# Leaving steps of a selective scan: clamp on VectorE, power first on GpSimd, gate ahead of the products

## The chip, the cores and the metric

One core of a Trainium2 chip runs the whole kernel. Its engines run side by side, each through its own queue in order: PE (TensorE, matrix products), DVE (VectorE), ACT (ScalarE), POOL (GpSimd) and SP (SyncE, which issues most DMAs). The metric is the device time of one execution in microseconds (us); the time shown for a kernel is the median of its runs.

## The reference

Eight images of 128 x 128 pixels with 128 channels go through two layers.

Layer 0 is linear attention: a projection to q, k and v, softmax of q over the head's dimension and of k over all pixels, a context matrix for each image, an output projection, a normalization over channels and a residual.

Layer 1 is a state-space block. `x @ Win` gives 256 channels `xb` and 256 gates `z`. `xb` goes through a 3 x 3 depthwise convolution and a SiLU. The result is read in four directions (by rows, backwards, by columns, columns backwards), and each direction has a scan over its 16384 positions:

```
state = exp(delta * A) * state + delta * u * B;   y = state * C
```

`delta` is a softplus of a small projection. The four directions' `y` are summed, with `u * D` added. What matters for the change is the end of the layer, for each pixel over its 256 channels:

```
yz  = y * silu(z)
var = mean(yz*yz) - mean(yz)^2             # over the channels
out = (gamma * (yz - mean) / sqrt(var + 1e-05) + beta) @ Wout
```

## The kernel before

Three stages run one after another: `layer0`, `layer1_front` (convolution, and all that the scans read, to DRAM) and `layer1_scan`. The change is in the last.

**Units and steps.** `layer1_scan` works through 512 units: eight output images, four directions each, 16 chunks of 1024 positions each. Channels lie on the 128 partitions, in two halves `c` = 0, 1. `step(n)` (L1100) issues unit n's scans, what follows the scans of unit n-1, and what leads to unit n+1. Everything is issued inside `in_order`, which ties each engine to the order in which `step` writes it: an engine never takes a later instruction first.

In a step without anything else, ACT makes the decay (`decay`, L937) and the softplus of the next unit (`soften`, L933); POOL multiplies u and delta into `h`, one half of the channels at a time (`weigh`, L946); DVE scans each half in place (`scan`, L954 forwards, L956 backwards); PE spreads C over the partitions into PSUM (`spread`, L962), once for each half chunk (512 positions); and DVE multiplies `h` by it (`emit`). For the first direction of an image the product writes straight into `y` (L974), the sum of the directions, which stays in SBUF for a whole image. For the other directions it takes three DVE operations (L984 or L988, `gather` L996, L977) and two additions on POOL (`add`, L1004).

`h` has two buffers, so `weigh(n, 0)` waits for the last reader of unit n-2's `h`: that is `scan(n-1, 1)`, which starts from its last column.

**Leaving steps.** When an image's four directions are summed, its 16 chunks leave, one a step, while the next image's first direction is scanned: steps 64 to 79 for the first image, and so on. The last image's chunks leave with no scan beside them. `leaving` says which chunk is at which step; in `step`, `now` is the chunk that leaves at this step, `last` the one before, `soon` the next. A chunk goes through this:

- `gate` (L1024) multiplies `y` by the stored `silu(z)`, in SBUF. Half 0 of a chunk is gated on POOL, at the end of the step before; half 1 on DVE, in the chunk's own step. (For the first chunk of an image both are on POOL.)
- `square` on ACT (L1027), `moments` on PE (L1037), `keep` on ACT (L1043), `to_tokens` on PE (L1049) and `square_mean` on ACT (L1053) give mean and mean square of each pixel.
- `variance` on DVE (L1057) subtracts the squared mean, from PSUM, at the end of the step, behind both scans. The tile `rstd` holds 8 values a partition.
- `project` on PE (L1069) multiplies the gated chunk by `Wout`, into the PSUM bank of the decay.
- `deviation(last)`, a step later, on POOL: the variance is clamped at 0 with 1e-5 added (L1061) and raised to the power -1/2 (L1062), in place.
- `store(last)` on DVE (L1075): eight instructions scale the projection by `rstd` and add the bias, into one of two buffers `r`, and SP sends each half chunk out (L1079).

So DVE's queue in a leaving step reads: product of the first half, gate of half 1, product of the other half, scan of half c = 0, eight store instructions, scan of c = 1, variance. POOL's reads: weighing c = 0, clamp, power, weighing c = 1, gate of the next chunk's half 0, and in two of three steps the issue of an accumulating DMA that adds `u * D` into `y` (`add_d`, L902). SP's reads: the rows of unit n+2 (L911, L912), z of a later chunk (L1020), `u` of unit n+2 in two halves (L918, each into a buffer that the weighing of unit n frees), and the two stores.

Of the kernel before, what the change touches and what calls it, by code (L numbers as in the profile page):

```python
# [11 lines left out]
ALU = mybir.AluOpType  # L12
# [22 lines left out]
EPS1 = 1e-5  # L35
# [707 lines left out]
def layer1_scan(ctx: ExitStack, tc, ubs, xps, zs, gs, dtw, dtb, a_log, gamma, beta, w_out, out):  # L743
# [15 lines left out]
    nc = tc.nc  # L759
# [144 lines left out]
    def load_rows(n):  # L904
        sl, i = units[n]
        m = sl.at(i)
        rw = rws[n % 3]
        md = NCH - 1 - m if sl.dt_turned_back else m
        src = xps[sl.dt_image, sl.dt_order].rearrange("j r l -> (j r) l")
        for j in range(3):  # L910
            nc.sync.dma_start(rw[3 * NR * j : 3 * NR * j + 3 * NR, :], src[:, md * CH : md * CH + CH])  # L911
        nc.sync.dma_start(rw[96:99, :], xps[sl.b, sl.order, :, R + 1, m * CH : m * CH + CH])  # L912

    def load(n, c):
        sl, i = units[n]
        m = sl.at(i)
        ubt[n, c] = wp.tile([P, CH], F32, name="ubt", tag="ub", bufs=4)
        nc.sync.dma_start(ubt[n, c], ubs[sl.b, sl.order, c][:, m * CH : m * CH + CH])  # L918
# [12 lines left out]
    def soften(n, c):  # L931
        sp[n, c] = t = wp.tile([P, CH], F32, name="sp", tag="sp", bufs=2)
        nc.scalar.activation(t, da[n, c], AF.Softplus)  # L933

    def decay(n, c):
        sl, i = units[n]
        nc.scalar.activation(da[n, c], sp[n, c], AF.Exp, scale=sa[:, sl.s, c : c + 1])  # L937

    def weigh(n, c):
        if c == 0:  # L940
            hs[n] = wp.tile([P, NC2, CH], F32, name="h", bufs=2)
        u, t, h = ubt.pop((n, c)), sp.pop((n, c)), hs[n][:, c, :]
        if units[n][0].permuted:
            u = u.rearrange("p (e h w) -> p h e w", e=2, w=W // 2)
            t, h = (v.rearrange("p (h e w) -> p h e w", e=2, w=W // 2) for v in (t, h))
        nc.gpsimd.tensor_tensor(h, u, t, ALU.mult)  # L946

    def scan(n, c):
        sl, i = units[n]
        x, e = da[n, c], hs[n][:, c, :]  # L950
        last = 0 if sl.back else CH - 1
        start = 0.0 if i == 0 else hs[n - 1][:, c, last : last + 1]
        if sl.back:
            nc.vector.tensor_tensor_scan(e[:, ::-1], x[:, ::-1], e[:, ::-1], start, ALU.mult, ALU.add)  # L954
        else:
            nc.vector.tensor_tensor_scan(e, x, e, start, ALU.mult, ALU.add)  # L956
# [7 lines left out]
    def emit(n, hf):  # L964

        sl, i = units[n]
        h = hs[n][:, :, hf * 512 : hf * 512 + 512]
        c = cps.pop((n, hf)).to_broadcast([P, NC2, GN])  # L970
        if sl.place == 0:
            v = sl.y_at(i, hf)
            split = "p c (a b) -> p c a b"
            nc.vector.tensor_tensor(v, h.rearrange(split, b=H), c.rearrange(split, b=H), ALU.mult)  # L974
            return
        if hf != sl.first:
            nc.vector.tensor_tensor(h, h, c, ALU.mult)  # L977
            return
        p = da.pop((n, 1))
        if sl.y_turned:  # L980
            ts[n] = p.rearrange("p (c b a) -> p c b a", c=NC2, a=GW)
            t = p.rearrange("p (c b a) -> p c a b", c=NC2, a=GW)
            split = "p c (a b) -> p c a b"
            nc.vector.tensor_tensor(t, h.rearrange(split, b=H), c.rearrange(split, b=H), ALU.mult)  # L984
        else:
            t = p.rearrange("p (c q) -> p c q", c=NC2)
            ts[n] = t.rearrange("p c (a b) -> p c a b", b=H)
            nc.vector.tensor_tensor(t, h, c, ALU.mult)  # L988

    def gather(n):  # L990

        sl, i = units[n]
        v = sl.y_at(i, sl.first)
        if sl.y_turned:
            v = v.rearrange("p c a b -> p c b a")
        nc.vector.tensor_tensor(v, v, ts.pop(n), ALU.add)  # L996
# [12 lines left out]
    def piece(m, hf):  # L1009
        return y[:, :, (2 * m + hf) * GN : (2 * m + hf + 1) * GN]  # L1010
# [5 lines left out]
    def fetch(o, m):  # L1016
        for hf in range(2):
            zt[m, hf] = z = wp.tile([P, NC2, GN], F32, name="z", bufs=6)
            p = mirrored(o, m, hf)
            nc.sync.dma_start(z, zs[o].rearrange("c p l -> p c l")[:, :, p * GN : p * GN + GN])  # L1020

    def gate(o, m, hf, eng):
        z, ym = zt[m, hf], piece(m, hf)
        eng.tensor_tensor(z, ym[:, :, ::-1] if o % 2 == 1 else ym, z, ALU.mult)  # L1024

    def square(m, hf):
        nc.scalar.activation(piece(m, hf), zt[m, hf], AF.Square)  # L1027

    def moments(m):

        pm = pe.tile([P, GN], F32, name="pm", tag="pt")
        for c in range(NC2):
            for j in range(2):
                for hf in range(2):
                    at = 32 * (2 * j + hf)
                    v = piece(m, hf) if j else zt[m, hf]
                    nc.tensor.matmul(pm[at : at + 32, :], mean, v[:, c, :], start=(c == 0), stop=(c == NC2 - 1))  # L1037
        pts[m, "rows"] = pm

    def keep(m):  # L1040
        pm = pts[m, "rows"]
        pts[m, "rows"] = sr = wp.tile([P, GN], F32, name="sr", bufs=1)
        nc.scalar.copy(sr, pm)  # L1043
# [11 lines left out]
    def variance(m):  # L1055
        rst[m] = rstd = sm.tile([P, GW, NC2], F32, name="rstd")
        nc.vector.tensor_tensor(rstd, pts.pop(m)[:, :, :, 1], mv.pop(m), ALU.subtract)  # L1057

    def deviation(m):
        rstd = rst[m]  # L1060
        nc.gpsimd.tensor_scalar(rstd, rstd, 0.0, EPS1, ALU.max, ALU.add)  # L1061
        nc.gpsimd.tensor_tensor(rstd, rstd, half, ALU.pow)  # L1062

    def project(m, hf, bank):
# [35 lines left out]
    def step(n):  # L1100
        live = 0 <= n < N
        then = n + 1 < N
        before = 1 <= n <= N
        now, last, soon, later = (leaving.get(n + i) for i in (0, -1, 1, 2))
        first = before and units[n - 1][0].place == 0
        if before:
            half1 = units[n - 1][0].first
            emit(n - 1, half1)
            if not first:
                gather(n - 1)  # L1110
        if now and last:
            gate(*now, 1, nc.vector)
        if before:
            emit(n - 1, 1 - half1)
        if n + 2 < N:
            load_rows(n + 2)
        if n in fetched:
            fetch(*fetched[n])
        if live:
            decay(n, 0)  # L1120
        if now:
            square(now[1], 1)
        if live:
            decay(n, 1)
            weigh(n, 0)
            if n + 2 < N:
                load(n + 2, 0)
        if last:
            deviation(last[1])
        if live:  # L1130
            weigh(n, 1)
            if n + 2 < N:
                load(n + 2, 1)
        if now:
            moments(now[1])
        if live:
            scan(n, 0)
            da.pop((n, 0))
        if last:
            for hf in range(2):  # L1140
                store(*last, hf)
        if then:
            for c in range(NC2):
                delta(n + 1, c)
        if now:
            keep(now[1])
        if then:
            soften(n + 1, 0)
        if now:
            to_tokens(now[1])  # L1150
            square_mean(now[1])
        if then:
            soften(n + 1, 1)
        if live:
            scan(n, 1)
        if first:
            hs.pop(n - 1)
        if now:
            variance(now[1])
        if live:  # L1160
            half1 = units[n][0].first
            spread(n, half1, "pc")
            spread(n, 1 - half1, "pt")
        if soon and now:
            gate(*soon, 0, nc.gpsimd)
        elif soon:
            gate(*soon, 1, nc.gpsimd)
        elif later:
            gate(*later, 0, nc.gpsimd)
        if soon:  # L1170
            square(soon[1], 0)
        if now:
            p = da.pop((n, 1)) if live else px.tile([P, CH], F32, name="px")
            for hf in range(2):
                project(now[1], hf, p[:, hf * 512 : hf * 512 + 512])
        elif live and units[n][0].place == 0:
            da.pop((n, 1))
        if before and not first:
            add(n - 1)
            hs.pop(n - 1)  # L1180
        if n in weighed:
            units[weighed[n]][0].weights()
        if n in summed:
            add_d(*summed[n])
# [78 lines left out]
```

## Time and profile before

| what | value |
|---|---|
| median of the runs shown (3) | 9363.71 us (9353.22 to 9363.73) |
| the profiled execution's own time | 9364.78 us |
| its span, first to last instruction | 9363.0 us |
| busy: PE / DVE / ACT / POOL | 6381.8 / 7997.6 / 7096.1 / 7319.3 us |
| scans: L954 and L956 | 1178.5 and 1177.8 us, 512 each, 2332 ns each |
| weighing: L946 on POOL | 2416.1 us, 1024, 2388 ns mean |
| gate: L1024 on DVE | 255.4 us, 120, 2128 ns mean; shortest 1214, longest 3367 |
| gate: L1024 on POOL | 329.7 us, 136, 2424 ns mean |
| clamp: L1061 on POOL | 143.3 us, 128; shortest 243, median 1209, longest 1640 ns |
| power: L1062 on POOL | 212.9 us, 128; 1657 to 1677 ns |
| variance: L1057 on DVE | 18.8 us, 128; 131 to 168 ns |

Busy time is the time in which an engine has an instruction under way; an instruction that has started and stands still counts as busy. The idle time before an instruction, with what ended it, stands behind it in square brackets. A row of a timeline with xN is N instructions on end.

From 5129 us on, the eight sets of leaving steps are where TensorE is busiest in the scan stage: 5129 to 5310, 5719 to 5900, 6306 to 6490, 6890 to 7070, 7473 to 7660, 8064 to 8250, 8655 to 8830, and the last image from 9233 to the end. In the first of them PE is busy for 146.70 of 181 us, DVE for 167.74, ACT for 139.09 and POOL for 155.81, and the DMA engines for a share of 0.89. A step of the other kind takes about 8.2 us (the first products L984 at 5328.88 and 5337.10).

### The profile page before, as it was taken

How to read it: one execution, taken by the hardware profiler on the slowest of the kernel's cores; microseconds unless marked ns; L12 is line 12 of the kernel's file. 1: busy time of each engine (PE TensorE's matmuls, PEld its weight loads, DVE VectorE, ACT ScalarE, POOL GpSimd, SP SyncE). 2: the span in 40 equal slices, each digit the busy share in tenths (PEclk: the TensorE clock that was granted, in tenths of full speed). 3: DMA queues.
4: the chain of work that ended last, by engine and by line, in shares of the span. 5: the costliest groups of instructions: out<-in, count | busy, mean ns of one | idle time of the engine just before them, and what ended most of it. 6: DMA issues, size and time to landing. Idle time of an engine off the chain costs nothing. (4 is left out here: it accounts for less than half of the span.)

```text
span 9363.0 us, 91413 instructions
## 1 busy us (share of the span) xinstructions
PE 6381.8 (68%) x24512; PEld 3145.7 (34%) x24512; DVE 7997.6 (85%) x7953; ACT 7096.1 (76%) x8066; POOL 7319.3 (78%) x4684
## 2 busy tenths in 40 slices
PE   8899998998888988888434636436364363643636
PEld 5555555554333333333101403114031140321403
DVE  6667666674799988888799999999999999999996
ACT  5555555658788888888688787887888878788885
POOL 3446444465688888888589899998999989999997
PEclk9999999999999999999655756657575575665857
DMA  1322333223477788888757759578595785967858
GB/s 75 144 91 90 134 118 144 105 80 143 159 240 239 249 233 230 234 233 225 215 155 208 234 169 260 166 204 239 167 267 166 206 234 165 252 175 200 248 165 216
DMA packets 934771, 1750.67 MB, mean 187 GB/s; under 512 B 150229, under 2 KB 376149, under 8 KB 926065
## 3 DMA queue, kind: packets, MB, share of 16 engines
q1 hardware_dynamic: 873328, 1509.92, 48.8%
q0 software_dynamic: 60928, 234.90, 13.5%
q8 instruction: 200, 3.28, 0.1%
q14 instruction: 315, 2.57, 0.1%
HBM read 1052.36 MB, written 692.12 MB: 186 GB/s over the span
## 5 line engine op out<-in xcount | busy, mean ns | idle before, releaser
L946 POOL TENSOR_TENSOR h<-ubt,sp 128x1024 f32<-128x1024 f32 x1024 | 2416.1, 2388 | 371.0 <-DMA rows<-xps 110.2
L929 PE MATMUL px<-rows,dtw 128*128 128x512 bf16 x2048 | 955.2, 565 | 2267.5 <-DVE y L996 1069.8
L525 POOL TENSOR_TENSOR tap<-tap 128x1024 f32<-128x1024 f32 x512 | 1211.2, 2366 | 299.1 <-ACT tap L523 278.8
L533 DVE SCALAR_TENSOR_TENSOR acc<-xb,cw,acc 128x1024 f32<-128x1024 f32 x1024 | 1320.6, 1290 | 76.1 <-ACT xb L502 28.2
L933 ACT ACTIVATE sp<-px 128x1024 f32<-128x1024 f32 x1024 | 1046.4, 1023 | 433.0 <-PE px L929 412.8
L929 PEld LDWEIGHTS <-dtw 128*128 128x128 bf16 x2048 | 168.3, 110 | 3090.0 <-issue 1019.3
L956 DVE TENSOR_TENSOR_SCAN h<-px,h 128x1024 f32<-128x1024 f32 x512 | 1177.8, 2332 | 32.0 <-ACT px L937 15.7
L954 DVE TENSOR_TENSOR_SCAN h<-px,h 128x1024 f32<-128x1024 f32 x512 | 1178.5, 2332 | 21.3 <-POOL h L946 18.4
L1004 POOL TENSOR_TENSOR y<-y,h 128x512 f32<-128x512 f32 x768 | 1158.6, 1550 | 3.9 <-DVE h L977 3.9
L515 PE MATMUL acc<-xi,wt 128*128 128x512 f32 x2048 | 985.4, 625 | 194.8 <-ACT ures L538 194.8
L937 ACT ACTIVATE px<-sp,sa 128x1024 f32<-128x1024 f32 x1024 | 1110.4, 1109 | 6.1
L523 ACT ACTIVATE tap<-xb,cw 128x1024 f32<-128x1024 f32 x768 | 825.2, 1140 | 16.7 <-POOL xb L499 16.5
L282 POOL TENSOR_TENSOR q<-q,qs 128x512 f32<-128x512 f32 x256 | 271.7, 1061 | 694.6 <-DVE qs L281 694.6
L933 ACT ACT_TABLE_LOAD x512 | 656.9, 1283 | 166.1 <-PE px L929 144.6
L937 ACT ACT_TABLE_LOAD x512 | 656.9, 1283 | 9.3
L515 PEld LDWEIGHTS acc<-xi,wt 128*128 128x128 f32 x2048 | 381.2, 196 | 772.0 <-issue 471.2
L1069 PEld LDWEIGHTS px<-wg,z 128*128 128x128 f32 x4096 | 595.9, 232 | 114.1 <-issue 108.0
L1069 PE MATMUL px<-wg,z 128*128 128x128 f32 x4096 | 594.3, 315 | 0.0
L962 PE MATMUL pc<-rows,csel 128*128 128x512 bf16 x1024 | 521.0, 589 | 75.0 <-DVE rstd L1057 71.1
L488 PE MATMUL pxb<-xi,wi 128*128 128x512 f32 x1024 | 487.2, 598 | 39.1 <-DMA xi<-x 36.9
L996 DVE TENSOR_TENSOR y<-y,px 128x1024 f32<-128x1024 f32 x384 | 468.7, 1221 | 14.4
L298 ACT ACTIVATE sq<-o 128x512 f32<-128x512 f32 x256 | 161.2, 630 | 421.4 <-DVE o L296 420.1
(153 smaller groups left out, 15040.3 us busy)
## 6 DMA issues: line engine op xcount, KB each, us to landing
ubt<-ubs SPq DMA_DIRECT2D x1024, 512.0 KB
zs<-z SPq DMA_DIRECT2D x512, 256.0 KB
ubs<-ures SPq DMA_DIRECT2D x256, 512.0 KB
ubs<-turned SPq DMA_DIRECT2D x256, 512.0 KB
z<-zs SPq DMA_DIRECT2D x256, 512.0 KB
y<-gs POOLq DMA_DIRECT2D x128, 1024.0 KB, 10.5
gs<-du POOLq DMA_DIRECT2D x96, 1024.0 KB, 8.8
rows<-xps SPq DMA_DIRECT2D x1536, 60.0 KB
```

Of the source, the lines that this page charges most:

```text
L515: nc.tensor.matmul(acc[:, s, :], wt[:, j, c, :], x, start=(j == 0), stop=(j == len(ON_PE) - 1))
L523: nc.scalar.activation(t, at(n, c, *d), AF.Copy, scale=weight(n, c, *d))
L525: nc.gpsimd.tensor_tensor(sums[n, c], sums[n, c], t, ALU.add)
L533: nc.vector.scalar_tensor_tensor(acc, at(n, c, *d), weight(n, c, *d), acc, ALU.mult, ALU.add)
L929: nc.tensor.matmul(p[:, hf * 512 : hf * 512 + 512], sl.dw[:, c * P : c * P + P], src, start=True, stop=True)
L933: nc.scalar.activation(t, da[n, c], AF.Softplus)
L937: nc.scalar.activation(da[n, c], sp[n, c], AF.Exp, scale=sa[:, sl.s, c : c + 1])
L946: nc.gpsimd.tensor_tensor(h, u, t, ALU.mult)
L954: nc.vector.tensor_tensor_scan(e[:, ::-1], x[:, ::-1], e[:, ::-1], start, ALU.mult, ALU.add)
L956: nc.vector.tensor_tensor_scan(e, x, e, start, ALU.mult, ALU.add)
L1004: nc.gpsimd.tensor_tensor(v[:, c], v[:, c], h[:, c], ALU.add)
L1069: nc.tensor.matmul(po[:, w, :], z[:, c, w * H : w * H + H], wg[:, c, :], start=(c == 0), stop=(c == NC2 - 1))
```

## The change

Three edits, all in the leaving steps:

1. The clamp with its added constant goes from `deviation` to `variance`: from POOL, ahead of the power, to DVE, behind the subtraction and one step earlier.
2. `deviation(last)`, which is now the power alone, is issued as the first thing of a step: POOL has it ahead of the first weighing, no longer behind it.
3. DVE's gate of half 1 is issued ahead of both products with C, no longer between them.

```diff
     def variance(m):
         rst[m] = rstd = sm.tile([P, GW, NC2], F32, name="rstd")
         nc.vector.tensor_tensor(rstd, pts.pop(m)[:, :, :, 1], mv.pop(m), ALU.subtract)
+        nc.vector.tensor_scalar(rstd, rstd, 0.0, EPS1, ALU.max, ALU.add)
 
     def deviation(m):
         rstd = rst[m]
-        nc.gpsimd.tensor_scalar(rstd, rstd, 0.0, EPS1, ALU.max, ALU.add)
         nc.gpsimd.tensor_tensor(rstd, rstd, half, ALU.pow)
...
         first = before and units[n - 1][0].place == 0
+        if last:
+            deviation(last[1])
+        if now and last:
+            gate(*now, 1, nc.vector)
         if before:
             half1 = units[n - 1][0].first
             emit(n - 1, half1)
             if not first:
                 gather(n - 1)
-        if now and last:
-            gate(*now, 1, nc.vector)
-        if before:
             emit(n - 1, 1 - half1)
...
             weigh(n, 0)
             if n + 2 < N:
                 load(n + 2, 0)
-        if last:
-            deviation(last[1])
         if live:
             weigh(n, 1)
```

## The prediction

> **What bounds the kernel now.** I read the page's busy table and slices first: VectorE (DVE) is busy 85% of the span and GpSimd (POOL) 78%, and in the scan stage, from 4700 us on, the table by stretches has DVE at 4423.7 and POOL at 4283.1 of 4663 us. The change touches only the leaving steps there: 16 for each of eight images, seven sets of them beside the next image's scans. So I read one of these steps in the timeline, first DVE alone, then POOL alone (columns: start, duration, engine, line, operation, operands, and idle time before it with what ended it).
>
> ```profile
> 5766.06 0.14 DVE L1057 TENSOR_TENSOR rstd<-pq,mv 128x8 f32<-128x8 f32 x1
> 5766.24 1.22 DVE L974 TENSOR_TENSOR y<-h,pc 128x1024 f32<-128x1024 f32 x1
> 5767.38 2.34 DVE L1024 TENSOR_TENSOR z<-y,z 128x1024 f32<-128x1024 f32 x1
> 5769.65 1.21 DVE L974 TENSOR_TENSOR y<-h,pc 128x1024 f32<-128x1024 f32 x1
> 5770.78 2.34 DVE L956 TENSOR_TENSOR_SCAN h<-px,h 128x1024 f32<-128x1024 f32 x1
> 5773.04 2.13 DVE L1075 SCALAR_TENSOR_TENSOR r<-px,rstd,bw 128x128 f32<-128x128 f32 x8
> 5775.09 2.34 DVE L956 TENSOR_TENSOR_SCAN h<-px,h 128x1024 f32<-128x1024 f32 x1
> 5777.35 0.14 DVE L1057 TENSOR_TENSOR rstd<-pq,mv 128x8 f32<-128x8 f32 x1
> ```
>
> ```profile
> 5766.29 2.36 POOL L946 TENSOR_TENSOR h<-ubt,sp 128x1024 f32<-128x1024 f32 x1
> 5768.63 1.21 POOL L1061 TENSOR_SCALAR rstd<-rstd 128x8 f32<-128x8 f32 x1
> 5769.92 1.67 POOL L1062 TENSOR_TENSOR rstd<-rstd,half 128x8 f32<-128x8 f32 x1
> 5771.56 2.35 POOL L946 TENSOR_TENSOR h<-ubt,sp 128x1024 f32<-128x1024 f32 x1
> 5773.89 2.34 POOL L1024 TENSOR_TENSOR z<-y,z 128x1024 f32<-128x1024 f32 x1
> 5776.18 1.27 POOL L902 DMA_DIRECT2D y<-gs  x1
> ```
>
> DVE has no gap: the step is DVE's chain, 11.29 us from variance to variance (V below is the variance's start). Two numbers are swollen. The gate (L1024) takes 2.34 us here and 1.22 in the last image, where no weighing is beside it; it ends at 5769.72, 1.07 after the weighing that was under way (5768.65). The clamp on POOL (L1061) takes 1.21 and ends at 5769.84, 0.12 after the gate; alone it takes 0.25. So the gate and a POOL operation do not overlap: each waits for the other to end. The first product of a leaving set shows the other order:
>
> ```profile
> 5720.76 1.60 DVE L1024 TENSOR_TENSOR z<-y,z 128x1024 f32<-128x1024 f32 x1
> 5721.34 3.24 POOL L946 TENSOR_TENSOR h<-ubt,sp 128x1024 f32<-128x1024 f32 x1
> ...
> 5724.62 2.35 DVE L956 TENSOR_TENSOR_SCAN h<-px,h 128x1024 f32<-128x1024 f32 x1 [1.13 <-POOL h L946]
> ```
>
> The weighing meets a gate, ends 2.22 after it, and the scan starts 0.04 after the weighing: that is the link that decides the change. In the steady step the first weighing ends at V+2.59 and its scan starts at V+4.72, so the link has 2.1 us to spare.
>
> **The change, part by part.** All offsets are from V, in a steady step.
>
> The clamp on DVE: one more 128x8 instruction. No DVE row shows it; the variance beside it takes 0.14 and the next starts 0.18 after it. I take 0.17, bounds 0.13 and 0.30 (98 steps: 4 us less, 13 more); POOL is idle then, since its part of the step ends at V+11.4. The gate, now next, starts at V+0.35.
>
> The gate ahead of both products: the weighing can't be under way any more, because POOL's queue now begins with the power, which waits for the clamp. So the gate takes 1.22 and its wait of 1.13 for the weighing goes; it ends at V+1.57. The two products need nothing that is late (their C rows and scans were ready), 1.14 each, so DVE stands at its first scan at V+3.8 instead of V+4.72.
>
> The power first on POOL is what pays for it. Queued behind it are both weighings, the other gate and the accumulating DMA (L902); the SP loads of later chunks wait for the weighings' buffers. Before, the first weighing started at V+0.23, on the end of the scan before. Now it starts after variance, clamp and power. The last image shows variance, gate and a woken POOL operation in just this order:
>
> ```profile
> 9339.38 0.17 DVE L1057 TENSOR_TENSOR rstd<-pq,mv 128x8 f32<-128x8 f32 x1 [1.66 <-ACT mv L1053]
> 9339.47 1.22 DVE L1024 TENSOR_TENSOR z<-y,z 128x1024 f32<-128x1024 f32 x1
> 9339.64 1.16 POOL L1061 TENSOR_SCALAR rstd<-rstd 128x8 f32<-128x8 f32 x1 [2.11 <-DVE rstd L1057]
> ```
>
> The gate starts 0.17 before POOL is awake, and POOL's small operation stands until 0.11 after the gate. The power would stand the same way: some 0.15 of it passes, then it waits until V+1.57, then its remaining 1.51: V+3.08. The weighing of 2.36 ends at V+5.42, the scan starts at V+5.46. From there to the next V nothing changes: 6.57 us (5770.78 to 5777.35). Sum: 0.35+1.22+1.51+2.34+0.04+6.57 = 12.03 against 11.28: **+0.75 us a step**. DVE now idles 1.65 us there. If the power got in first, the gate would stand for it and the weighing for both; the sum is the same. The unshown cost is the power beside a gate: no row has the two together. If it is not held, the weighing ends at V+4.41 (start V+0.41, 1.64, 2.36), the scan starts at V+4.45, and the step is 11.02: −0.26. So the bounds are −0.26 and +0.75; I take the upper, since the clamp row, same engine, tile and neighbour, is held to the end.
>
> The Trainium skill, "SBUF — State Buffer", section "Who interferes with whom", says that a VectorE instruction with two SBUF inputs and a GpSimd one that reads SBUF exclude each other for the whole instruction, and that issue order decides who stands. Its advice to let the operation off the critical path stand is what this change gets wrong by that rule; the sum by it is 12.03 too. It also says that a tensor_scalar between SBUF tiles may take a two-port mode and then contend with any GpSimd operation. No run here shows it on this clamp.
>
> Edges of each set of 16. First step: POOL is still in its additions until V+1.75, so gate, power and weighing follow one another from there: the gate ends at V+2.85 as now, the scan starts at V+6.74 instead of 5.11: +1.63. Second step: 12.31 now, because POOL was late; 12.03 after: −0.28. The step after the last: no gate, the power ends at V+2.1, the second scan starts about 0.97 later. With 13 steady steps an image pays 1.63−0.28+13×0.75+0.97 = 12.1, seven images 84.5 us. The last image's steps (7.35 us) go by TensorE's projection, the moments behind it and ScalarE; gate, clamp and power have over 0.7 us of slack there: nothing.
>
> What gives some back: the output buffers.
>
> ```profile
> DVE r L1075 <- DMA out<-r: 71.9, 29, 8.4
> ```
>
> That is the waits' row (total, times, longest) for the store waiting for its earlier DMA. By windows, 39.1 us of it fall in the seven sets beside scans (9.1, 6.0, 5.2, 1.8, 7.9, 9.1, 0), with 3.1 more put down to POOL's gate; the rest is in the last image. DMA share stands at 1.0 to 1.07 in those steps, so a longer step takes load off it. Each stretch with stalls gets 11 steps × 0.75, about 8.5 us, to catch up. Bounds: nothing given back, or all 42. I take three quarters, 30 us, because the stalled steps are followed by quick ones (14.84 after 10.94), as queues do that catch up.
>
> **Sum**: 84.5−30 = +54.5 us on the profiled execution's own 9364.78 us (span 9363.0): 9419. The median of the runs shown is 9363.71, one us lower, so the same within what can be told.
>
> **Rivals.**
> 1. The power is not held by the gate and runs beside it. Then −0.26 in 13 steps, +0.7 and −1.3 in the first two, +1.0 after the last: −3.0 an image, −21 us: 9344, and up to 9360 where DMA takes it back. For it: nothing shows the power beside a gate, and most of its 1.66 us is arithmetic. Against it: it must read first, and the clamp row stands. It decides for faster from the point where the first weighing ends before V+4.68.
> 2. DMA gives nothing back, or the later weighing holds SP's in-order loads (the weighing's end, which frees the buffer, goes from V+2.6 to V+5.4), and stores wait longer: 84.5 plus up to 20: 9449 to 9470. For it: DMA is full there. Against: SP reaches that load only at V+4.7 today.
> 3. All 42 us of stalls go, and the edges (7 × 2.3 = 16 us) hide in them too: 84.5−42−16 = +26, 9391; with what else DMA may catch up, 9384 to 9405. For it: the quick steps. Against: image seven's set has no stall to lose.
>
> **Numbers.** Forecast 9419, own range 9405 to 9449: 0.65. Rival 1 0.13 (0.08 faster by over 0.2%, 0.05 within). Rival 2 0.12. Rival 3 0.10, of which 0.02 within 0.2%. A measurement of this kernel can tell about 0.2%, 19 us, from no change. So faster 0.08, same 0.07, slower 0.85. The range of 8 in 10 takes rival 3 and the lower half of rival 2: 9385 to 9455; outside stay rival 1 and the top of rival 2.
>
> **What would show it.** Right: the gate on DVE at about 1.22 us in all leaving steps; steps of about 12.0 us; a new idle of about 1.6 us before the first scan (L954, L956), released by POOL's weighing, some 100 times; the power's rows at about 2.6 us instead of 1.66; fewer waits for out<-r. Wrong: powers at 1.66 beside a gate of 1.22 and steps near 11.0 (rival 1); out<-r waits above 72 us (rival 2); or a variance that comes later, so that the power, and all behind it, waits for ScalarE.

## The result, and the profile after

The changed kernel takes 9414.69 us (median of 6 runs, 9401.54 to 9421.95) against 9361.99 (6 runs, 9353.22 to 9373.65): a ratio of 1.0055, with a 95% interval from 1.0042 to 1.0068. It is slower by some 53 us; forecast were +54.5. The profiled execution took 9401.54 us (span 9399.8), which is the lowest of the six, and 36.8 more than that of before.

The line of busy times on the page after is a lesson in itself: VectorE and GpSimd are both *less* busy than before (7997.6 and 7319.3), and the kernel is slower.

```profile
PE 6401.6 (68%) x24512; PEld 3145.0 (33%) x24512; DVE 7913.9 (84%) x8081; ACT 7095.6 (75%) x8066; POOL 7276.6 (77%) x4556
```

An instruction that stands counts as busy. The 120 gates on VectorE no longer stand (255.4 us before, 1.22 each now), which takes away some 110 us of "busy"; what came in their place is idle time. On GpSimd the clamp's 143.3 us went, and the power's standing came (212.9 us before, 320.1 now). A steady leaving step of after, VectorE's timeline first (columns as in the prediction), then GpSimd's:

```profile
5755.44 0.14 DVE L1057 TENSOR_TENSOR rstd<-pq,mv 128x8 f32<-128x8 f32 x1
5755.61 0.17 DVE L1058 TENSOR_SCALAR rstd<-rstd 128x8 f32<-128x8 f32 x1
5755.69 1.22 DVE L1024 TENSOR_TENSOR z<-y,z 128x1024 f32<-128x1024 f32 x1
5756.83 2.35 DVE L974 TENSOR_TENSOR y<-h,pc 128x1024 f32<-128x1024 f32 x2
5760.77 2.35 DVE L956 TENSOR_TENSOR_SCAN h<-px,h 128x1024 f32<-128x1024 f32 x1 [1.60 <-POOL h L946]
5763.04 2.13 DVE L1075 SCALAR_TENSOR_TENSOR r<-px,rstd,bw 128x128 f32<-128x128 f32 x8
5765.09 2.34 DVE L956 TENSOR_TENSOR_SCAN h<-px,h 128x1024 f32<-128x1024 f32 x1
5767.35 0.14 DVE L1057 TENSOR_TENSOR rstd<-pq,mv 128x8 f32<-128x8 f32 x1
```

```profile
5755.86 2.55 POOL L1062 TENSOR_TENSOR rstd<-rstd,half 128x8 f32<-128x8 f32 x1 [2.39 <-DVE rstd L1058]
5758.38 4.67 POOL L946 TENSOR_TENSOR h<-ubt,sp 128x1024 f32<-128x1024 f32 x2
```

The gate takes 1.22 us. The power starts 0.17 after it and ends at 5758.41, 1.50 after the gate's end (5756.91). Only then does the weighing begin, and the scan stands 1.60 us for it. From variance to variance: 11.91 us, before 11.28.

The waits (total us, times, longest) show the same over the whole kernel. Before, the first two rows were 18.4 in 12 waits and 15.1 in 10, and the stores' 71.9 in 29.

```profile
DVE h L954 <- POOL h L946: 118.3, 72, 2.2
DVE h L956 <- POOL h L946: 90.2, 55, 2.2
DVE r L1075 <- DMA out<-r: 36.5, 16, 6.7
```

And the power's group on the page (busy total and mean ns of one, then idle before): 1663 ns was its mean before.

```profile
L1062 POOL TENSOR_TENSOR rstd<-rstd,half 128x8 f32<-128x8 f32 x128 | 320.1, 2501 | 268.7 <-DVE rstd L1058 267.9
```

Where the 36.8 us of the two profiled executions lie, from the variances' starts in the two traces:

| stretch | before | after | difference |
|---|---|---|---|
| up to the first leaving set | 5129.0 | 5125.3 | -3.7 |
| the seven sets beside scans, first to last variance | 1245.7 | 1277.6 | +31.9 |
| between the sets, last to next first variance | 2858.9 | 2868.0 | +9.1 |
| last image | 129.4 | 128.9 | -0.5 |

The first row has nothing to do with the change. Up to the first scan of the stage, all fourteen kernels of this document do the same work, and in their profiled executions that scan starts between 4599.11 and 4615.95 us (4610.84 before, 4607.02 after). So a single execution can differ from another by up to 17 us before any step is reached.

### The profile page after: what moved, and what is told of

Its sections match the earlier page's. It is cut to its first block, busy times and chain, and to the rows that moved or that the text cites. A ratio compares the mean times of both kernels' runs of the same rounds, so it can differ in the third digit from the quotient of the medians.

```text
span 9399.8 us, 91321 instructions
## 1 busy us (share of the span) xinstructions
PE 6401.6 (68%) x24512; PEld 3145.0 (33%) x24512; DVE 7913.9 (84%) x8081; ACT 7095.6 (75%) x8066; POOL 7276.6 (77%) x4556
## 5 line engine op out<-in xcount | busy, mean ns | idle before, releaser
L1062 POOL TENSOR_TENSOR rstd<-rstd,half 128x8 f32<-128x8 f32 x128 | 320.1, 2501 | 268.7 <-DVE rstd L1058 267.9
## 6 DMA issues: line engine op xcount, KB each, us to landing
y<-gs POOLq DMA_DIRECT2D x128, 1024.0 KB, 10.3
```

## The experiments

**Theory**: the step got longer because GpSimd's power, put first and standing for the gate, delays the weighing that the scan needs; the stores' waits give part of it back. **Rivals**: the clamp on VectorE alone costs it; the stores' waits decide whatever the steps do; the power's length has no part in it. Each kernel stands beside runs of before on the same chip: 9363.92 us for the first four, 9371.39 for the next four, 9367.58 for the last four. A step is meant without stalls, from variance to variance, unless it says otherwise. A set is the 15 steps from an image's first variance to its last.

**The clamp alone** (edit 1 of the change).

```diff
     def variance(m):
...
+        nc.vector.tensor_scalar(rstd, rstd, 0.0, EPS1, ALU.max, ALU.add)
 
     def deviation(m):
         rstd = rst[m]
-        nc.gpsimd.tensor_scalar(rstd, rstd, 0.0, EPS1, ALU.max, ALU.add)
```

> Only the first edit: the clamp on VectorE behind the variance; power and gate where they were before. Theory (the gate and a GpSimd operation exclude each other, and the cost of the change is that power and gate stand ahead of the first weighing, whose end starts the scan): the weighing still starts at V+0.2, so only VectorE's queue grows, by 0.08 to 0.17 us in a step: steps of 11.36 to 11.45, about +8 to +16 us before the stores give some back: 9362 to 9378 us. Rival A (the instruction added to the bound engine, and its own standing for GpSimd, are the cost): most of the +53 us is here already, 9395 or more.

9381.39 us, ratio 1.002 (1.0011 to 1.0028): a third of the whole change's cost, 3 us above the expected range. The steady step is 11.29, unchanged: the gate stands for a weighing either way, and 0.08 more ahead of it is 0.06 less in it (2.28 us). What the trace shows of the rest are steps whose variance came late. VectorE, then GpSimd:

```profile
8706.67 0.17 DVE L1057 TENSOR_TENSOR rstd<-pq,mv 128x8 f32<-128x8 f32 x1 [0.55 <-ACT mv L1053]
8706.87 1.76 DVE L1058 TENSOR_SCALAR rstd<-rstd 128x8 f32<-128x8 f32 x1
```

```profile
8706.25 2.36 POOL L946 TENSOR_TENSOR h<-ubt,sp 128x1024 f32<-128x1024 f32 x1 [3.73 <-issue]
```

The weighing had begun, and the clamp, 0.17 us elsewhere, ends 0.02 after it (8708.63 against 8708.61). Such a step takes 11.84 instead of 10.94. So a small operation on VectorE with one input stands too. In this execution, the slowest of the twelve, 27 of the 112 clamps of the seven sets stand, and the stores' waits there are 46.8 us against 39.1; how the two share the 17 us of the medians isn't settled.

**The gate alone** (edit 3), everything else as before.

```diff
         first = before and units[n - 1][0].place == 0
+        if now and last:
+            gate(*now, 1, nc.vector)
         if before:
             half1 = units[n - 1][0].first
             emit(n - 1, half1)
             if not first:
                 gather(n - 1)
-        if now and last:
-            gate(*now, 1, nc.vector)
-        if before:
             emit(n - 1, 1 - half1)
```

> Only the third edit: VectorE's gate ahead of both products; clamp and power stay on GpSimd between the weighings. Theory: the gate starts at V+0.18, just ahead of the weighing (V+0.23), so it takes 1.22 us and the weighing stands until V+1.4 and ends at V+3.6; the scan starts at V+3.65 instead of 4.72. VectorE's part of a step would be 10.2 us, but GpSimd's queue (11.2 to 11.4 us with the DMA issue, in two of three steps) and the full DMA hold it: steps of 10.2 to 11.3, so 9310 to 9360 us. Rival B (the gate's new place is what costs, because it delays the products): 9390 or more.

9364.06 us, ratio 0.9997 (0.9989 to 1.0006): no difference, 4 us above the expected range. Yet the commonest step without a stall is quicker by 0.84. Two steps of one set, VectorE and then GpSimd:

```profile
5762.28 2.93 DVE L1024 TENSOR_TENSOR z<-y,z 128x1024 f32<-128x1024 f32 x1
...
5773.96 0.14 DVE L1057 TENSOR_TENSOR rstd<-pq,mv 128x8 f32<-128x8 f32 x1
5774.02 1.21 DVE L1024 TENSOR_TENSOR z<-y,z 128x1024 f32<-128x1024 f32 x1
```

```profile
5761.77 2.36 POOL L946 TENSOR_TENSOR h<-ubt,sp 128x1024 f32<-128x1024 f32 x1 [5.05 <-issue]
...
5774.19 3.27 POOL L946 TENSOR_TENSOR h<-ubt,sp 128x1024 f32<-128x1024 f32 x1 [1.28 <-ACT mv L1053]
```

Where the gate starts first it takes 1.21, the weighing stands instead, and the step is 10.44 if no store waits. Where the weighing is first, in 31 of 105 steps, the gate stands: mostly for 2.93 us in all, as here, in a step of 11.77 without a stall, or for 3.34 in one of 12.17. The quick steps then meet the stores, whose waits rise to 97.5 us from 71.9:

```profile
DVE r L1075 <- DMA out<-r: 97.5, 36, 6.3
```

**The clamp and the gate** (edits 1 and 3), with the power where it was.

> First and third edit; the power stays behind the first weighing. Theory: as the gate alone, with 0.3 us less on GpSimd and 0.08 to 0.17 more on VectorE: 9300 to 9355 us, faster than before; the +53 us must then come from the power's place. Rival A: 9395 or more. Rival B: 9390 or more.

9426.14 us, ratio 1.0069 (1.0057 to 1.0081): the expectation fell, on the wrong side. The step is 12.41, nearly all through the seven sets. VectorE, GpSimd:

```profile
8725.93 0.14 DVE L1057 TENSOR_TENSOR rstd<-pq,mv 128x8 f32<-128x8 f32 x1
8726.10 0.17 DVE L1058 TENSOR_SCALAR rstd<-rstd 128x8 f32<-128x8 f32 x1
8726.18 3.41 DVE L1024 TENSOR_TENSOR z<-y,z 128x1024 f32<-128x1024 f32 x1
8729.51 2.34 DVE L974 TENSOR_TENSOR y<-h,pc 128x1024 f32<-128x1024 f32 x2
8731.77 2.34 DVE L954 TENSOR_TENSOR_SCAN h<-px,h 128x1024 f32<-128x1024 f32 x1
```

```profile
8726.15 2.36 POOL L946 TENSOR_TENSOR h<-ubt,sp 128x1024 f32<-128x1024 f32 x1 [1.63 <-ACT mv L1053]
8728.47 2.64 POOL L1062 TENSOR_TENSOR rstd<-rstd,half 128x8 f32<-128x8 f32 x1
```

The clamp moves the gate's start from V+0.06 to V+0.25; the weighing starts at V+0.22. By 0.03 us the gate comes second and stands 2.2 us on the path. In one step the weighing came late (8851.32 us, the gate at 8851.06): there the gate takes 1.23 and the step 10.44. So the power in front is not only a cost of the change: it is what keeps the weighing behind the gate. The prediction had that for the changed kernel; the expectation of this run forgot it.

**The clamp and the power first** (edits 1 and 2), the gate still between the products:

```diff
         first = before and units[n - 1][0].place == 0
+        if last:
+            deviation(last[1])
...
             weigh(n, 0)
...
-        if last:
-            deviation(last[1])
         if live:
             weigh(n, 1)
```

> First and second edit: clamp on VectorE, power first on GpSimd; the gate stays between the two products. Theory: the power runs alone from V+0.42 to V+2.08, the gate (ready at V+1.4) stands for it. If the gate then has the port, the weighing ends at V+5.4 as in the changed kernel: steps of 11.9, 9395 to 9425 us. If the weighing has it, the gate ends at V+5.5 and the scan starts behind the second product at V+6.6: steps of 13.1, 9480 to 9550 us. Rival B: without the gate's move the kernel is near before, 9360 to 9380 us.

9412.64 us, ratio 1.0052 (1.004 to 1.0064): as slow as the whole change, so edits 1 and 2 are enough for its loss. It lies inside the expected range of 9395 to 9425, but not for the reason given: the steps say something that the expectation and the prediction had denied. VectorE, GpSimd:

```profile
8732.70 0.14 DVE L1057 TENSOR_TENSOR rstd<-pq,mv 128x8 f32<-128x8 f32 x1
...
8734.08 1.22 DVE L1024 TENSOR_TENSOR z<-y,z 128x1024 f32<-128x1024 f32 x1
8735.22 1.21 DVE L974 TENSOR_TENSOR y<-h,pc 128x1024 f32<-128x1024 f32 x1
8737.57 2.35 DVE L954 TENSOR_TENSOR_SCAN h<-px,h 128x1024 f32<-128x1024 f32 x1 [1.14 <-POOL h L946]
```

```profile
8733.13 1.66 POOL L1062 TENSOR_TENSOR rstd<-rstd,half 128x8 f32<-128x8 f32 x1 [1.23 <-DVE rstd L1058]
8734.77 5.09 POOL L946 TENSOR_TENSOR h<-ubt,sp 128x1024 f32<-128x1024 f32 x2
```

The gate starts 0.95 us into the power, while it is still under way, and neither stands: 1.22 and 1.66 us, their times alone. Only the weighing behind stands for the gate, for some 0.4. The scan starts at V+4.87 and a step without a store's wait takes 11.46, shorter than the 11.92 of the whole change. The time is the same because the stores' waits come back (73.7 us in 34 waits against 36.5 in 16).

**What the stores give back**: before, after and the gate alone, each sending only half 0 of every chunk. Half of the output is left out; the scaling instructions remain.

```diff
-        nc.sync.dma_start(dst[:, s, :], r)
+        if hf == 0:
+            nc.sync.dma_start(dst[:, s, :], r)
```

> The kernel before, with the second half chunk of each output computed but not sent (half of the output is left out), so that a store hardly waits for an earlier one. Theory (part of the cost of 70 us that the steps show was given back by the stores, whose waits shrank): the seven sets beside scans fall to 170.9 us each, as the seventh has now, and the last image loses most of its 33 us of waits: 9275 to 9310 us. Rival C (the waits for the stores are not what gave anything back; they only lie where other waits would): less than 25 us are gained, 9340 or more.

> The changed kernel, with the second half chunk of each output not sent. Theory: it has little left to lose beside scans (steps are 11.92 already), so it gains the last image's 25 us and some 10 more: 9365 to 9390 us, and the distance to the kernel before with the same cut is 70 to 85 us, where it is 53 with all stores. Rival C: the distance stays at 45 to 60 us.

> The gate alone ahead of the products (clamp and power on GpSimd in their old places), second half chunk not sent. Theory: its steps of 10.44 us, seen in the run of the gate alone, are no longer stretched by stores; with one step in three of about 12 us, where the weighing is ahead of the gate, the sets come to some 165 us: 9225 to 9275 us, 20 to 60 below the kernel before with the same cut. Rival D (GpSimd's queue, not the stores, took the gate's gain): equal to the kernel before with the same cut, within 15 us.

Before 9315.1 us (5 above its range), after 9388.02 (inside), the gate alone 9283.12 (8 above). The stores' waits of the first and second:

```profile
DVE r L1075 <- DMA out<-r: 12.5, 7, 4.7
```

```profile
DVE r L1075 <- DMA out<-r: 5.0, 4, 3.4
```

The steps are what they were (11.28, 11.92; 10.44 with some of 12.17), but now they decide. After is 72.9 us above before, not 52.7, so the stores hide about 20 us of the steps' cost in the medians, which rest on four to ten executions each and leave some 10 us either way. In the two profiled executions the sets differ by 1269.7-1199.1 = 70.5 and the stretches between by 8.9. The gate alone is 32 us below before's 9315.1, where with all stores it gained nothing: the stores' waits had taken that gain. With half the output they are 22.1 us in 13 waits, with all of it 97.5 in 36.

**A multiplication in the power's place**, in after with half the output. The result's scale is another one; only the time is of interest.

```diff
-        nc.gpsimd.tensor_tensor(rstd, rstd, half, ALU.pow)
+        nc.gpsimd.tensor_tensor(rstd, rstd, half, ALU.mult)
```

> The changed kernel with a multiplication in place of the power (same tile, same place, same waits; the normalization is left out), second half chunk not sent. Theory (the power's 1.6 us, in line behind the gate and ahead of the weighing, is the cost): the weighing starts at V+1.6, the scan at V+3.95, steps of 10.5 us: 9200 to 9260 us, over 120 below the changed kernel with the same cut. Rival A or B (clamp or the gate's place): within 40 us of it.

9317.31 us: 71 us below the same kernel with the power, where more than 120 was expected (its range ended at 9260), and more than the 40 of the rivals. The step without a stall hit: 10.48 us against 11.92. GpSimd's row:

```profile
8734.48 1.10 POOL L1062 TENSOR_TENSOR rstd<-rstd,half 128x8 f32<-128x8 f32 x1 [1.69 <-DVE rstd L1058]
```

It starts 0.18 after its gate (8734.30, 1.23 us) and ends 0.05 after it, where the power ends 1.50 after. So the delay of the weighing is the wait for the gate and then the power's own length. The missing 50 us went to the stores again: 68.8 us in 34 waits, though they send half; 56.1 of it lie in the seven sets, where the kernel with the power has 0.7. Why they wait so much longer than in the gate alone (22.1), whose quick steps are as short, stays open.

**The accumulating DMAs two steps earlier**, alone and with the gate alone. `summed` says in which step GpSimd issues each `add_d` (L902); the DMA engines have a share of 0.89 over the first set before.

```diff
-            summed[n - NCH + 3 + (3 * j + 1) // 2] = e
+            summed[n - NCH + 1 + (3 * j + 1) // 2] = e
```

> The kernel before, with the 16 accumulating DMAs of u*D into y issued two steps earlier for each image (all still issued, at the same density), so that one or two fewer of them fall into a set of leaving steps. Theory (DMA is full in the first eleven leaving steps, and stores wait for it there; one accumulating DMA takes some 5 us of all 16 engines): the 42 us of store waits beside scans shrink by half to three quarters: 9325 to 9350 us. Rival C (the waits are the stores' own latency, whatever else is sent): within 10 us of the kernel before.

> The gate alone ahead of the products, with the sums issued two steps earlier. Theory: the gate's steps of 10.44 us were paid back to store waits; with 7 us less of DMA in a set some of that is kept: 9300 to 9345 us, below the kernel before and the changed one, and 10 to 40 below the same with the gate in its old place. Rival D: no better than the kernel before with the sums earlier.

Alone: 9355.0 us, ratio 0.9987 (0.9978 to 0.9996); less than expected, and the theory's reason fell: the stores' waits stayed (78.6 us in 39), and in the seven sets they rose from 39.1 to 53.4. In the profiled execution the first scan already starts 10.3 us earlier than before (4600.51 against 4610.84), where the kernels are still the same, so no part of the gain is shown to come from the steps. With the gate: 9323.82 us, ratio 0.9954 (0.9941 to 0.9966), inside the expected range and faster than both kernels. How the two share the gain isn't settled: the medians say 0, -13 and -44 us for gate, sums and both, while the sets of the profiled executions of the gate alone and of both differ by only 2 us (1231.5, 1229.3).

**The gate ahead of the variance**: VectorE gates the next chunk's half 1 behind the second scan, where GpSimd does not weigh, and takes the variance after it; clamp and power as before. Once alone, once with the sums earlier.

```diff
             if not first:
                 gather(n - 1)
-        if now and last:
-            gate(*now, 1, nc.vector)
-        if before:
             emit(n - 1, 1 - half1)
...
+        if now and soon:
+            gate(*soon, 1, nc.vector)
         if now:
             variance(now[1])
```

> VectorE's gate of the next chunk at the end of the step, between the second scan and the variance; clamp and power on GpSimd between the weighings as before. Theory (who starts first has the port, and the gate waits for a weighing that has started): the gate now starts at the scan's end, always some 0.2 us ahead of the weighing, also where the variance waits for ScalarE, so no gate takes over 1.3 us beside scans and the 12.2 us steps of the gate alone go; the stores' waits still take most of it: 9335 to 9365 us. Rival E (the gate there delays the variance and with it TensorE's second spread and the projection): 9380 or more.

> The gate between the second scan and the variance, and the sums issued two steps earlier. Theory: quick steps of about 10.4 us without the 12.2 us ones, and less DMA in the sets: the best of all, 9290 to 9340 us. Rival C: 9355 or more.

9442.49 us, ratio 1.0079 (1.0065 to 1.0093), and 9403.31, ratio 1.0037 (1.0025 to 1.005): the theory missed both, the rival was right, and the first is the slowest kernel of the study. The gate takes 1.20 in most steps, as meant. But TensorE's next spread of C waits for the variance, and that now comes a gate later; the waits of the first of the two:

```profile
PE pc L962 <- DVE rstd L1057: 184.7, 112, 4.2
...
DVE r L1075 <- DMA out<-r: 125.2, 51, 9.6
DVE h L954 <- ACT px L937: 59.9, 60, 1.8
DVE r L1075 <- PE px L1069: 53.3, 35, 6.1
```

Before, the first row was 71.1 us, in 94 waits. TensorE's projection is later (the last row), and the decays as well. A wait was taken away, and the queue behind it moved the loss to TensorE.

## Why the prediction was right, step by step

**The mechanism** held in the steady steps: the gate at 1.22, the power held to the gate's end plus 1.50 (1.51 forecast), the weighing behind it, a new idle of 1.6 us ahead of the first scan, 105 waits more than before ("some 100"). The step is 11.92 where 12.03 was forecast, +0.64 instead of +0.75. The 0.1 too much is the gate's start: V+0.35 was taken, it starts at V+0.25, 0.08 after the clamp has started.

**The edges** were of the right size for a partly wrong reason. The first step of a set has +1.9 (11.95 to 13.84 in the mean of seven) against +1.63. Only the gate was to stand for GpSimd's additions there; in fact the clamp already does. After, VectorE and GpSimd:

```profile
5716.79 1.82 DVE L1058 TENSOR_SCALAR rstd<-rstd 128x8 f32<-128x8 f32 x1
5718.52 1.21 DVE L1024 TENSOR_TENSOR z<-y,z 128x1024 f32<-128x1024 f32 x1
```

```profile
5715.26 3.31 POOL L1004 TENSOR_TENSOR y<-y,h 128x512 f32<-128x512 f32 x2
5718.68 2.57 POOL L1062 TENSOR_TENSOR rstd<-rstd,half 128x8 f32<-128x8 f32 x1
```

The clamp ends 0.04 after the additions. The Trainium skill, "SBUF — State Buffer", section "Who interferes with whom", lists this form, a tensor_scalar, among those that can enter a mode with two ports, when its operands meet the mode's conditions, and then contend with GpSimd. The prediction noted that no run showed it; the clamp's 1.82 here and 1.76 with the clamp alone agree with it. The second step saved 0.07, not 0.28; the step after the last cost 1.3 (9.1 us over seven stretches), not 0.97.

**The cost without stores** was forecast as 84.5 us. With half the output the profiled pair differs by 79.4 (70.5 and 8.9), the medians by 72.9.

**What the stores give back** was the least certain term: 30 us, between 0 and 42. The stores' waits in the seven sets fell from 39.1 to 5.3 us in the profiled pair, whose sets and the stretches between them differ by 41.0 in all: 79.4-41.0 = 38 given back. In the medians it is 72.9-52.7, about 20. Thirty lies between. Its ground was thin: in "14.84 after 10.94" the stalled step comes behind the quick one, though that quick step does follow a stalled one, of 14.30. So +54.5 met the medians' +52.7 with two errors of opposite sign, a cost some 10 too high (84.5 against 72.9) and a return some 10 too high; that they cancel is luck. The median lies in the stated range, 9405 to 9449, but the sum was made on a profiled execution, and the profiled execution after is 18 us below the sum (9401.54 against 9419), outside that range and inside rival 3's 9384 to 9405.

**A side remark was wrong**: "If the power got in first, the gate would stand for it and the weighing for both; the sum is the same." With the gate between the products the power is first, the gate does not stand, and the step is 0.46 shorter (11.46 against 11.92). The remark took the rule of exclusion for the whole length of any instruction. The forecast didn't rest on it, as the gate starts first in the changed kernel.

**The rivals.** The power beside a gate without standing (rival 1) does occur in these runs, but only where the power starts first. Rival 2, nothing given back, falls with the stores' waits going down. Rival 3, all stalls and edges hidden, has the waits for it (5.3 us left in the sets) and the edges against it (9.1 us stayed between the sets).

## What to carry to other kernels

Where two engines exclude each other, write down for each pair who starts first and by how much: 0.03 us decided between steps of 10.44 and 12.41. A step is only worth what the next limit leaves of it; taking half the stores out showed both the loss (73 for 53 us) and the gain (32 for 0) that the stores' waits had covered. And an operation moved to the front of a queue is paid by everything behind it, even where it frees its neighbour.

## What the runs showed of the hardware that was not expected

- A power on GpSimd (128x8, 1.66 to 1.68 us in the kernel before) that has begun does not hold a VectorE gate that starts 0.95 us later (1.22 us); a power that starts 0.17 after the gate stands to the gate's end and then takes its 1.50. A multiplication of the same tiles in the same place ends 0.05 after the gate. That the power is done reading by then would fit; it wasn't tried by itself. The Trainium skill's page "SBUF — State Buffer", section "Who interferes with whom", says that a VectorE instruction with two SBUF inputs contends with a GpSimd one that reads SBUF; for this pair it agrees with one order and not with the other.
- A VectorE clamp of 128x8, 0.17 us alone, stands for a GpSimd weighing or addition that has begun: 1.76 and 1.82 us.
- The bytes alone don't set the waits of the stores for their DMA: with the same half of the output they are 12.5 us at steps of 11.28, 5.0 at 11.92, and 68.8 at 10.48. The steps' length alone doesn't either: the gate alone has quick steps of 10.44 and waits of 22.1.
